# Last blocks of the last attention group straight to TensorE, and the last 512 rows in two interleaved halves

## The chip, the cores and the metric

The kernel runs on one core of one Trainium2 chip. The metric is the time of the device in microseconds (us), lower is better. The core has four computing engines, each with a queue of its own that is worked off in order: TensorE (PE) multiplies matrices, VectorE (DVE) and ScalarE (ACT) work element by element and read the results of TensorE from PSUM, GpSimd (POOL) works element by element in SBUF. SyncE (SP) only issues DMAs; GpSimd issues DMAs as well, among them those that add what they carry to their destination. Engines wait for one another by semaphores.

## The reference

One layer of graph attention over 8 frames of 2048 rows with 256 channels, 8 heads of 32 channels, and a mask that is the same for all frames:

```python
scores = jnp.einsum('fnhd,fmhd->fhnm', q, k) / jnp.sqrt(jnp.asarray(D, x.dtype))
mask = (adj > 0)[None, None, :, :]
scores = jnp.where(mask, scores, jnp.asarray(-1000000000.0, x.dtype))
attn = jax.nn.softmax(scores, axis=-1)
t = jnp.einsum('fhnm,fmhd->fnhd', attn, v).reshape(F, N, C)
x = _layernorm(x + t, ln1_g, ln1_b)
h = jax.nn.relu(jnp.einsum('fnc,cd->fnd', x, w1) + b1)
f_out = jnp.einsum('fnd,dc->fnc', h, w2) + b2
x = _layernorm(x + f_out, ln2_g, ln2_b)
...
x = _layernorm(x + _L0_gnn_ref(x, adj, ...), axis=-1)
```

So each row passes three layer norms: after the attention (with the input added), after the feed-forward part, and after the input has been added once more. All is in float32.

## The kernel before, in words

The queries are taken in chunks of 512 rows, `qc`, four to a frame. A chunk is done in two groups `g` of four heads, and a group in 16 blocks `mb` of 128 keys. So there are 8 x 4 x 2 x 16 = 1024 items. The main loop has one step for each item:

- `scores` of the item two steps ahead: four matmuls on TensorE (L230), and two operations of VectorE that add the mask and write the tile `p` (L233);
- `exponentials` of the item one step ahead: one activation of ScalarE in place (L237);
- `values` of this item: four matmuls that add up over the group's 16 blocks in PSUM (L249);
- `add_up`: the softmax sums. The 16 tiles `p` of a group are first added to each other: blocks 3, 6, 8, 11, 13, 15 onto block 0 by GpSimd (L271, `POOLED`), blocks 4, 7, 10 onto 1 and 5, 9, 12 onto 2 by DMAs that GpSimd issues (L268, `MOVED`); block 14 stays alone. `denominator` then multiplies the four tiles that are left with ones on TensorE (L310), a "term" of four matmuls each. In the very last group blocks 13 and 15 are terms of their own (`ENDED`), six terms in all. The sum is copied by ScalarE (`dT`, L312), transposed, and VectorE takes the reciprocal.

All else is written as generators, kept in a list `fill` with a start step and a due step. Before each step `advance` resumes them: `yield BANK` asks for a PSUM bank, and is granted when TensorE has credit left in the step or the earliest due step has come; `yield n` waits n steps; only one generator holds the spare bank. The program's text so made is the order of every engine's queue; nothing is reordered later.

`outcome` divides a chunk's attention by its sums (L345), and GpSimd issues a DMA that adds the input rows to y (L334). `tail` follows: the first norm (`norm`: statistics on VectorE, L278 and L279; power and products on GpSimd, L282 to L286; scaling on ScalarE, L289), `feed_forward` (transposes, the activation L410 that writes `turned`, W1 on TensorE with a relu on ScalarE, L423, W2 with a sum on VectorE, L436; y times g1 and plus be1 and b2 on GpSimd, L412 and L414), the second norm, g2 and be2 on GpSimd (L355, L357), a DMA that adds the input again (L359), the third norm, and the output DMA by SyncE (L362). A tail may start 10 steps after a chunk's `outcome` could, and is due 16 steps later. It thus runs in the next chunk's loop, except for what is left of the second-last chunk's tail when the loop ends.

The last chunk has `finish` in the place of `outcome` and `tail`. Its norms are done by `norm_halves`, two row tiles after the other two (statistics L372, L373; GpSimd L375, L376; L378 makes the bias `nb`; scaling L382), but its feed-forward part takes the four tiles at once. The input rows are loaded eight steps before the loop's end. `finish` has no points at which it gives way to the tail after its feed-forward part, so the last part of that tail is recorded behind all of `finish`.

Of the kernel before, what the change touches and what calls it, by code (L numbers as in the profile page):

```python
# [10 lines left out]
F32 = mybir.dt.float32  # L11
# [8 lines left out]
P = 128  # L20
# [41 lines left out]
def fast_path(ctx, tc, cst, x, adj, out, RS):  # L62
# [52 lines left out]
    def take(shape, dt):  # L115
        live.pop(0)
        live.append(ld.tile(shape, dt, name="in"))
        return live[-1]
# [139 lines left out]
    MOVED = ((1, 4, 7, 10), (2, 5, 9, 12))  # L258
    ALONE = 14

    ENDED = (13, 15)
    SUM = 4

    def add_up(item):
        f, qc, g, mb = item
        for chain in MOVED:
            if mb in chain[1:]:
                nc.gpsimd.dma_start(PT[f, qc, g, chain[0]], PT.pop(item), accum_op=ALU.add)  # L268
        if mb in POOLED[1:] and not ((f, qc, g) == items[-1][:3] and mb in ENDED):
            first = PT[f, qc, g, POOLED[0]]  # L270
            nc.gpsimd.tensor_tensor(first, first, PT.pop(item), ALU.add)  # L271


    def norm(t):
        mv = small.tile([P, TPC, nc.vector.BN_AGGR_DIM], F32, name="mv")
        for j in range(TPC):
            st = small.tile([P, nc.vector.BN_STATS_DIM], F32, name="st")
            nc.vector.bn_stats(st, t[:, j, :])  # L278
            nc.vector.bn_aggr(mv[:, j, :], st)  # L279
            yield 1  # L280
        rs = small.tile([P, TPC], F32, name="rs")
        nc.gpsimd.tensor_scalar(rs, mv[:, :, 1], EPS, 1.0, op0=ALU.add, op1=ALU.mult)  # L282
        nc.gpsimd.tensor_tensor(rs, rs, cst["mhalf"], ALU.pow)  # L283
        nb = small.tile([P, TPC], F32, name="nb")
        nc.gpsimd.tensor_tensor(nb, mv[:, :, 0], rs, ALU.mult)
        nc.gpsimd.tensor_scalar(nb, nb, -1.0, 1.0, op0=ALU.mult, op1=ALU.mult)  # L286
        yield 2
        for j in range(TPC):
            nc.scalar.activation(t[:, j, :], t[:, j, :], AF.Identity, bias=nb[:, j:j + 1], scale=rs[:, j:j + 1])  # L289
            yield 1  # L290

    def rows(v):
        return v[:, None, :].to_broadcast([P, TPC, C])

    def denominator(f, qc, g, ready):
        grp = (f, qc, g)
        terms = [PT.pop((f, qc, g, ALONE))] + [PT.pop((f, qc, g, chain[0])) for chain in MOVED + (POOLED,)]
        if (f, qc, g) == items[-1][:3]:
            terms[3:3] = [PT.pop((f, qc, g, b)) for b in ENDED]
        yield BANK  # L300
        ps = bank()
        for n, term in enumerate(terms):
            if n:
                yield MORE
            while n == len(terms) - 1 and state["now"] < ready:
                yield WAIT
            state["credit"] -= 4 * CH
            for h in range(4):
                r = D * h
                nc.tensor.matmul(ps[r:r + D, :], cst["ones"], term[:, h, :], start=(n == 0), stop=(n == len(terms) - 1))  # L310
        dT = op.tile([P, CH], F32, name="dT")
        nc.scalar.copy(dT, ps)  # L312
        yield 1
        yield BANK
        ps = bank()
        transposes(ps, [dT[:, j::TPC] for j in range(TPC)])
        if g == 0:
            RC[f, qc] = op.tile([P, TPC, H], F32, name="rc")
        rc = RC[f, qc]
        den = ps.rearrange("p (j c) -> p j c", c=P)[:, :, ::D]  # L320
        nc.vector.reciprocal(rc[:, :, 4 * g:4 * g + 4], den)
        nc.vector.tensor_tensor(RS[:, 0], RS[:, 0], den, ALU.add)
        nc.vector.tensor_tensor(RS[:, 1], RS[:, 1], den, ALU.min)
        if g == 1:
            begin = items.index((f, qc, g, LAST)) + SUM + 2
            start(begin, outcome(f, qc) if (f, qc) != (F - 1, NCK - 1) else finish(f, qc), begin)

    def outcome(f, qc):
        yield ROOM
        state["tails"] += 1  # L330
        xin = x[f, qc * CH:(qc + 1) * CH, :].rearrange("(p j) c -> p j c", p=P)
        y = yp.tile([P, TPC, C], F32, name="y")
        yield from divide(f, qc, y)
        nc.gpsimd.dma_start(y, xin, accum_op=ALU.add)  # L334
        begin = items.index((f, qc, 1, LAST)) + SUM + 2
        start(begin + 10, tail(f, qc, y, xin), begin + 26)

    def divide(f, qc, y):
        rc = RC.pop((f, qc))
# [6 lines left out]
                                    ps.rearrange("p (j h d) -> p j h d", h=4, d=D),  # L346
                                    rc[:, :, 4 * gg:4 * gg + 4, None].to_broadcast([P, TPC, 4, D]), ALU.mult)

    def tail(f, qc, y, xin):
        yield from norm(y)  # L350
        yield from feed_forward(y)
        yield 1
        z = y
        yield from norm(z)
        nc.gpsimd.tensor_tensor(z, z, rows(cst["g2r"]), ALU.mult)  # L355
        yield 1
        nc.gpsimd.tensor_tensor(z, z, rows(cst["be2r"]), ALU.add)  # L357
        yield 1
        nc.gpsimd.dma_start(z, xin, accum_op=ALU.add)  # L359
        yield 7  # L360
        yield from norm(z)
        nc.sync.dma_start(out[f, qc * CH:(qc + 1) * CH, :].rearrange("(p j) c -> p j c", p=P), z)  # L362
        state["tails"] -= 1


    def norm_halves(t):
        both = []
        for h in range(0, TPC, 2):
            mv = small.tile([P, 2, nc.vector.BN_AGGR_DIM], F32, name="mv")
            for j in range(2):  # L370
                st = small.tile([P, nc.vector.BN_STATS_DIM], F32, name="st")
                nc.vector.bn_stats(st, t[:, h + j, :])  # L372
                nc.vector.bn_aggr(mv[:, j, :], st)  # L373
            rs = small.tile([P, 2], F32, name="rs")
            nc.gpsimd.tensor_scalar(rs, mv[:, :, 1], EPS, 1.0, op0=ALU.add, op1=ALU.mult)  # L375
            nc.gpsimd.tensor_tensor(rs, rs, cst["mhalf"][:, 0:2], ALU.pow)  # L376
            nb = small.tile([P, 2], F32, name="nb")
            nc.vector.scalar_tensor_tensor(nb, mv[:, :, 0], -1.0, rs, op0=ALU.mult, op1=ALU.mult)  # L378
            both.append((h, rs, nb))
        for h, rs, nb in both:  # L380
            for j in range(2):
                nc.scalar.activation(t[:, h + j, :], t[:, h + j, :], AF.Identity, bias=nb[:, j:j + 1], scale=rs[:, j:j + 1])  # L382

    def finish(f, qc):
        y = yp.tile([P, TPC, C], F32, name="y")
        xr, xb = state["rows"], take([P, TPC, C], F32)
        yield from divide(f, qc, y)
        nc.vector.tensor_tensor(y, y, xr, ALU.add)
        norm_halves(y)
        nc.vector.tensor_tensor(xb, xr, rows(cst["be2r"]), ALU.add)  # L390
        yield from feed_forward(y)
        z = y
        norm_halves(z)
        for h in range(0, TPC, 2):
            nc.vector.tensor_tensor(z[:, h:h + 2], z[:, h:h + 2], rows(cst["g2r"])[:, h:h + 2], ALU.mult)
            nc.vector.tensor_tensor(z[:, h:h + 2], z[:, h:h + 2], xb[:, h:h + 2], ALU.add)
        norm_halves(z)
        dst = out[f, qc * CH:(qc + 1) * CH, :].rearrange("(p j) c -> p j c", p=P)
        for h in range(0, TPC, 2):
            nc.sync.dma_start(dst[:, h:h + 2], z[:, h:h + 2])  # L400

    def feed_forward(y):
        yield TURNED
# [37 lines left out]
    def start(t, gen, due):  # L441
        fill.append([t, gen, 1, due])
        fill.sort(key=lambda e: e[3])
# [108 lines left out]
    for t, (f, qc, g, mb) in enumerate(items):  # L552
        if g == 1 and mb % 2 and (f + 1 < F or qc + 1 < NCK):
            load_mask(f + (qc + 1) // NCK, (qc + 1) % NCK, mb // 2)
        for what, *which in NEXT.get(t % FRAME, []):
            to = f if what is ask and which[0] else f + 1
            if to < F:
                at = (0, 0, 0) if what is turn else (which[0], 0, 0) if what is ask else (0, which[1], which[0] * TPC)
                start(t, what(to, *which), t + 3 * MB if what is turn else items.index((to, *at)) - LEAD - 1)
        if t == len(items) - MB // 2:  # L560
            state["rows"] = take([P, TPC, C], F32)
            nc.sync.dma_start(state["rows"], x[f, qc * CH:(qc + 1) * CH, :].rearrange("(p j) c -> p j c", p=P))
        if t:
            advance(t)

        if t + 1 < len(items):
            exponentials(items[t + 1])
        if t + LEAD < len(items):
            nf, _, ng, nmb = items[t + LEAD]
            t0 = t  # L570
            while (nf, nmb // TPC, ng) not in V:
                advance(t0, finish=True)
                t0 += 1
            scores(items[t + LEAD])
        values(items[t])
        add_up(items[t])
        if mb == LAST:
            start(t + 2, denominator(f, qc, g, t + SUM), t + SUM + 4)
    t = len(items)
    state["side"] = None  # L580
    while fill:
# [238 lines left out]
```

## Time and profile before

| what | us |
|---|---|
| median of 3 runs | 3248.77 (3247.61 to 3251.02) |
| profiled execution, its own time | 3242.05 |
| its span | 3240.0 |
| mask addition on VectorE, L233, mean of 2048 | 1.219 |
| exponential on ScalarE, L237, mean of 1024 | 1.910 |
| addition on GpSimd, L271, mean of 382 | 4.791 |
| DMA p<-p, median from issue to landing, 384 of them | 10.5 |
| DMA y<-in_x_dram, the same, 62 of them | 8.0 |

The span is the time from the first to the last instruction of one profiled execution; times of day below are from the start of this span. A line of the timeline gives start, length, engine, line, operation, the tile written and the tiles read, how many instructions are merged in it, and in brackets how long the engine was idle before and who ended the wait. "x8" in matmul lines counts the records of four matmuls in float32. The chain of waits goes back from the last instruction, at each step to what released it. A line such as L54 is a helper's, so W1 and W2 are told apart by the tiles read: `turned,w1s` and `w2s,hT`.

### The profile page before, as it was taken

The page shows a single profiled execution, that of the slowest core. Times are in us where ns is not written, and L with a number is a line of the kernel's source. Part 1 is how long each engine was busy: PE and PEld are TensorE (multiplying, and loading weights), DVE is VectorE, ACT ScalarE, POOL GpSimd, SP SyncE. Part 2 cuts the span into 40 slices and gives each one's busy share as a digit, 9 for nine tenths or more (in the row PEclk, how much of TensorE's full clock was granted, in tenths as well). Part 3 has the DMA queues.
Part 4 walks back from the last instruction along what each step waited for, and adds up shares of the span by engine and source line. Part 5 has one row for each costly group of instructions (what it writes and reads, how often), then busy time and mean ns, then how long its engine had stood idle before and what let it go on. Part 6 is the DMA issues. An engine that isn't in the chain of part 4 may idle for free.

```text
span 3240.0 us, 68306 instructions
## 1 busy us (share of the span) xinstructions
PE 3101.0 (96%) x28948; PEld 976.0 (30%) x28948; DVE 2739.5 (85%) x3203; ACT 2435.5 (75%) x1937; POOL 2593.3 (80%) x1357
## 2 busy tenths in 40 slices
PE   7899999999999999999999999999999999998994
PEld 4222333323332233322333323323233323332221
DVE  4888888888888888888988888888888888888994
ACT  3667778778778777778777778777778777777773
POOL 0568888788878888788887888888888788878894
PEclk8899999999999999999999999999999999999997
DMA  9688779778879788788788879878788878877773
GB/s 322 147 179 190 182 175 202 176 174 200 181 176 205 171 190 193 158 195 200 177 181 175 184 181 220 177 167 197 175 192 194 180 171 201 181 171 160 168 160 78
DMA packets 153384, 591.57 MB, mean 183 GB/s; under 512 B 15056, under 2 KB 67792, under 8 KB 103920
## 3 DMA queue, kind: packets, MB, share of 16 engines
q0 software_dynamic: 64560, 435.85, 67.2%
q1 hardware_dynamic: 87696, 149.98, 13.1%
q8 instruction: 229, 3.75, 0.4%
q10 hardware_dynamic: 816, 1.31, 0.1%
q14 instruction: 83, 0.68, 0.1%
HBM read 146.67 MB, written 37.75 MB: 57 GB/s over the span
## 4 chain that ended last, share of the span: by engine, by line
PE 75%; DVE 8%; POOL 5%; DMA 4%; issue 4%; ACT 2%; DVEq 0%; ACTq 0%; POOLq 0%
PE s L230 28%; PE x L249 24%; PE x L54 13%; DVE p L233 6%; PE x L310 6%; PE x L95 4%; DMA p<-p 3%; POOL p L271 2%; ACT p L237 2%; DMA mask<-md 1%; POOL y L357 1%; DVE st L278 1%; POOL y L355 0%; POOL y L414 0%; POOL y L412 0%
## 5 line engine op out<-in xcount | busy, mean ns | idle before, releaser
L233 DVE TENSOR_TENSOR p<-s,mask 128x1024 f32<-128x1024 f32 x2048 | 2410.5, 1219 | 360.3 <-PE s L230 202.9
L237 ACT ACTIVATE p<-p 128x2048 f32<-128x2048 f32 x1024 | 1956.3, 1910 | 510.2 <-DVE p L233 456.7
L271 POOL TENSOR_TENSOR p<-p 128x2048 f32<-128x2048 f32 x382 | 1829.5, 4791 | 216.0 <-ACT p L237 213.8
L230 PE MATMUL s<-qT,kT 32*128 32x512 f32 x8192 | 1171.2, 641 | 34.1 <-DVE p L233 29.1
L249 PE MATMUL x<-p,v 128*32 128x512 f32 x8192 | 1092.9, 606 | 16.7 <-ACT p L237 16.7
L268 POOL DMA_DIRECT2D p<-p x384 | 360.1, 957 | 305.5 <-ACT p L237 95.5
L230 PEld LDWEIGHTS s<-qT,kT 32*128 32x128 f32 x8192 | 320.5, 183 | 637.8 <-DVE p L233 580.1
L249 PEld LDWEIGHTS x<-p,v 128*32 128x32 f32 x8192 | 161.3, 108 | 796.4 <-issue 302.6
L310 PE MATMUL x<-p,ones 128*32 128x512 f32 x2016 | 261.1, 594 | 15.9 <-POOL p L271 9.7
L289 ACT ACTIVATE y<-y,nb,rs 128x256 f32<-128x256 f32 x372 | 219.2, 590 | 46.1 <-POOL nb L286 46.1
L54 PE MATMUL x<-in,wqkv 128*32 128x512 f32 x1888 | 243.5, 592 | 0.0
L278 DVE BATCH_NORM_STATS2 st<-y 128x6 f32<-128x256 f32 x372 | 155.2, 417 | 6.2 <-DMA y<-in_x_dram 6.2
L54 PE MATMUL x<-w2s,hT 128*32 128x256 f32 x2048 | 122.8, 381 | 3.3 <-DVE y L436 2.3
L54 PE MATMUL x<-turned,w1s 128*32 128x512 f32 x992 | 122.9, 592 | 0.4 <-ACT in L166 0.4
L54 PEld LDWEIGHTS x<-wqkv,in 128*32 128x32 f32 x3584 | 102.2, 110 | 63.5 <-issue 59.0
L54 PE MATMUL x<-wqkv,in 128*32 128x128 f32 x3584 | 117.2, 273 | 0.0
L310 PEld LDWEIGHTS x<-p,ones 128*32 128x32 f32 x2016 | 64.1, 110 | 171.4 <-issue 136.0
L54 PEld LDWEIGHTS x<-in,wqkv 128*32 128x32 f32 x1888 | 61.7, 110 | 140.9 <-issue 113.7
L283 POOL TENSOR_TENSOR rs<-rs,mhalf 128x4 f32<-128x4 f32 x93 | 97.1, 1044 | 7.7
L54 PEld LDWEIGHTS x<-w2s,hT 128*32 128x32 f32 x2048 | 66.1, 110 | 76.5 <-issue 30.3
L414 POOL TENSOR_TENSOR y<-y,be1b2r 128x1024 f32<-128x1024 f32 x32 | 85.4, 2667 | 0.6
L355 POOL TENSOR_TENSOR y<-y,g2r 128x1024 f32<-128x1024 f32 x31 | 82.7, 2668 | 1.2 <-ACT y L289 1.2
(117 smaller groups left out, 1333.1 us busy)
## 6 DMA issues: line engine op xcount, KB each, us to landing
p<-p POOLq DMA_DIRECT2D x384, 1024.0 KB, 10.5
in<-xd SPq DMA_DIRECT2D x87, 512.0 KB, 10.7
mask<-md SPq DMA_DIRECT2D x248, 128.0 KB, 8.0
y<-in_x_dram POOLq DMA_DIRECT2D x62, 512.0 KB, 8.0
p<-in_adj_dram SPq DMA_DIRECT2D x16, 1024.0 KB, 9.7
out_dram<-y SPq DMA_DIRECT2D x31, 512.0 KB, 6.4
in<-in_x_dram SPq DMA_DIRECT2D x29, 512.0 KB, 15.9
xd<-in SPq DMA_DIRECT2D x28, 512.0 KB, 10.9
```

Of the source, the lines that this page charges most:

```text
L54: nc.tensor.matmul(out[r:r + D], lhsT[:, r:r + D], rhs, start=start, stop=stop)
L95: nc.tensor.transpose(ps[:, j * P:(j + 1) * P], s, ident)
L230: nc.tensor.matmul(ps2[half][:, j, :], KT[f, mb // TPC, g][r:r + D, (mb % TPC) * P:(mb % TPC + 1) * P], QT[f, qc, g][r:r + D, :], start=Tr ...
L233: nc.vector.tensor_tensor(pt[:, 2 * half:2 * half + 2, :], ps, MK[f, qc, mb // 2][:, mb % 2, None, :].to_broadcast([P, 2, CH]), ALU.add)
L237: nc.scalar.activation(PT[item], PT[item], AF.Exp, scale=1.0 / math.sqrt(D))
L249: nc.tensor.matmul(O[grp][r:r + D, :], V[f, mb // TPC, g][:, mb % TPC, r:r + D], PT[item][:, h, :], start=(mb == 0), stop=(mb == LAST))
L268: nc.gpsimd.dma_start(PT[f, qc, g, chain[0]], PT.pop(item), accum_op=ALU.add)
L271: nc.gpsimd.tensor_tensor(first, first, PT.pop(item), ALU.add)
L278: nc.vector.bn_stats(st, t[:, j, :])
L283: nc.gpsimd.tensor_tensor(rs, rs, cst["mhalf"], ALU.pow)
L289: nc.scalar.activation(t[:, j, :], t[:, j, :], AF.Identity, bias=nb[:, j:j + 1], scale=rs[:, j:j + 1])
L310: nc.tensor.matmul(ps[r:r + D, :], cst["ones"], term[:, h, :], start=(n == 0), stop=(n == len(terms) - 1))
```

## The change

It has three parts, and touches only the last group and the last two chunks.

1. In the last group blocks 11 to 15 are not added up: no GpSimd addition of block 11, no DMA of block 12. `denominator` has eight terms there instead of six, in the order 0, 11, 12, 2, 13, 14, 1, 15, each with the step before which it must not come, and it starts three steps before the loop's end and not two steps after.
2. The second-last chunk's tail may start 5 steps after its `outcome` could (10 before) and is due 3 steps later (16 before). Its norms do two row tiles to a step (`per=2`) instead of one.
3. `finish` makes two generators `half_rows`, for two row tiles each, and resumes them in turn through all stages: norm, products, transposes, W1, W2, norm, g2 and be2, norm, output DMA. The products with g1 and the sum with be1 and b2 go to tiles of the input rows. The input rows plus be2 (`xb`) are made by GpSimd two steps before the loop's end, where VectorE made them in `finish`.

```diff
-    ENDED = (13, 15)
+    ENDED = MB - 5
...
-            if mb in chain[1:]:
+            if mb in chain[1:] and not ((f, qc, g) == items[-1][:3] and mb >= ENDED):
...
-        if mb in POOLED[1:] and not ((f, qc, g) == items[-1][:3] and mb in ENDED):
+        if mb in POOLED[1:] and not ((f, qc, g) == items[-1][:3] and mb >= ENDED):
...
-        terms = [PT.pop((f, qc, g, ALONE))] + [PT.pop((f, qc, g, chain[0])) for chain in MOVED + (POOLED,)]
+        blocks = [ALONE] + [chain[0] for chain in MOVED + (POOLED,)]
+        late = {len(blocks) - 1: ready}
         if (f, qc, g) == items[-1][:3]:
-            terms[3:3] = [PT.pop((f, qc, g, b)) for b in ENDED]
+            blocks = [POOLED[0], 11, 12, MOVED[1][0], 13, 14, MOVED[0][0], 15]
+            late = {n: len(items) - k for n, k in ((2, 2), (3, 1), (4, 1), (5, 0), (6, 0), (7, 0))}
...
-        start(begin + 10, tail(f, qc, y, xin), begin + 26)
+        if (f, qc) == (F - 1, NCK - 2):
+            start(begin + 5, tail(f, qc, y, xin, 2), begin + 8)
+        else:
+            start(begin + 10, tail(f, qc, y, xin), begin + 26)
...
+    def half_rows(h, y, xr, xb, yT, hT, dst):
...
+        nc.vector.tensor_tensor(y, y, xr, ALU.add)
+        if h:
+            yield
+        found = half_stats(y)
+        yield
+        half_norm(y, *found)
+        nc.gpsimd.tensor_tensor(xr, y, row2(cst["g1r"]), ALU.mult)
+        nc.gpsimd.tensor_tensor(xr, xr, row2(cst["be1b2r"]), ALU.add)
+        yield
+        ps = bank()
+        transposes(ps, [y[:, j, a * P:(a + 1) * P] for a in range(2) for j in range(2)])
+        for a in range(2):
+            nc.scalar.activation(yT[:, a, q], ps[:, a * 2 * P:(a + 1) * 2 * P], AF.Identity,
+                                 bias=cst["be1c"][:, a:a + 1], scale=cst["g1c"][:, a:a + 1])
+        yield
...
+            nc.scalar.activation(hT[:, d, q], ps[:, d * 2 * P:(d + 1) * 2 * P], AF.Relu, bias=cst["b1s"][:, d:d + 1], scale=1.0)
+        yield
...
+        nc.vector.tensor_tensor(z, ps.rearrange("p (b c) -> p b c", c=C), xr, ALU.add)
+        found = half_stats(z)
+        yield
+        half_norm(z, *found)
+        yield
+        nc.vector.tensor_tensor(z, z, row2(cst["g2r"]), ALU.mult)
+        nc.vector.tensor_tensor(z, z, xb, ALU.add)
+        found = half_stats(z)
+        yield
+        half_norm(z, *found)
+        nc.sync.dma_start(dst[:, own], z)
...
+        both = [half_rows(h, y, xr, xb, yT, hT, dst) for h in range(2)]
+        while both:
+            for e in list(both):
+                if next(e, both) is both:
+                    both.remove(e)
...
+        if t == len(items) - 2:
+            nc.gpsimd.tensor_tensor(xb, xr, rows(cst["be2r"]), ALU.add)
...
-        if mb == LAST:
+        if mb == LAST and t + 1 < len(items):
             start(t + 2, denominator(f, qc, g, t + SUM), t + SUM + 4)
+        if t == len(items) - 3:
+            start(t, denominator(f, qc, g, t), t)
```

`half_stats` and `half_norm` are the statistics and the scaling of `norm_halves`, for one half each.

## The prediction

> **What bounds the kernel now.** The page's first part:
>
> ```profile
> span 3240.0 us, 68306 instructions
> PE 3101.0 (96%) x28948; PEld 976.0 (30%) x28948; DVE 2739.5 (85%) x3203; ACT 2435.5 (75%) x1937; POOL 2593.3 (80%) x1357
> ```
>
> These shares are those of a long uniform loop and say nothing on its end, where the change lies. The built program of the changed kernel has the same instructions in the same order on all engines up to block 11 of the group before the last, so only the last 128 us of the span can change. There the chain of work that ended last is:
>
> ```profile
> 3173.61 2.30 POOL y L414
> 3175.91 7.17 DMA p<-p
> 3183.12 3.69 PE s L310 x32
> 3186.83 0.59 ACT dT L312
> ...
> 3220.96 2.32 POOL y L357
> 3223.27 0.29 issue
> 3223.56 5.85 DMA y<-in_x_dram
> 3229.44 0.44 DVE st L278
> ```
>
> (start, length, what.) The last multiplication with the values starts at 3173.88, but its softmax sums reach ScalarE (dT) only at 3186.83: they wait for the add of block 12, whose DMA GpSimd issues late, behind additions. From there to the end of the span lie 53.2 us: the last 512 rows, and after them the tail of the 512 rows before, which waits for L357 and its DMA. Then the timeline of the loop:
>
> ```profile
> 3084.36 1.06 PE L249 MATMUL x<-p,v 128*32 128x512 f32 x8
> ...
> 3085.24 1.91 PE L54 MATMUL x<-w2s,hT 128*32 128x256 f32 x32
> ...
> 3088.15 1.07 PE L249 MATMUL x<-p,v 128*32 128x512 f32 x8
> ...
> 3112.27 4.83 DVE L233 TENSOR_TENSOR p<-s,mask 128x1024 f32<-128x1024 f32 x4
> ...
> 3112.65 0.86 POOL L334 DMA_DIRECT2D y<-in_x_dram  x1 [1.49 <-DVE y L345]
> ...
> 3117.29 4.84 DVE L233 TENSOR_TENSOR p<-s,mask 128x1024 f32<-128x1024 f32 x4 [0.19 <-ACT y L289]
> ```
>
> DVE adds the mask back to back, a block in 2.4 to 2.5 us: a plain step is DVE's. In a step that also holds 16 matmuls of 256 columns TensorE is the limit: 3088.15 - 3084.36 = 3.79 us. So a step costs max(2.5, 2.05 + TensorE's extra work), plus DVE's extra work where DVE limits. The instructions of L334 in a window around its last issue answer:
>
> ```profile
> DMA to landing us min/median/max: 9.6/9.6/9.6
> ```
>
> Those rows of y are complete at 3112.65 + 9.6 = 3122.25.
>
> **What the Trainium skill says.** "DMA: Bandwidth & Descriptors", section Queues, rings and completion order: each DMA engine consumes descriptors in ring order. The trace agrees: L334's transfer, behind a 1 MB p<-p transfer issued at 3110.25, took 9.6 us; the same kind at 3223.56, with nothing ahead, took 5.9. "TensorE: Matmul & The Clock Gate", Part 1: idle for about 3.4 us halves the clock, about 3.4 us of work restores it. The stretches of two us agree; the number before the last two is the granted clock:
>
> ```profile
> 3188.00:3190.00 2.00, 1.19 (x10) 0.99 (x9) 1.75 (x9) 0.00 (x0) 0.00 (x0) 1.00 0.00 0
> 3192.00:3194.00 2.00, 0.00 (x0) 0.00 (x0) 1.27 (x5) 0.00 (x0) 0.44 (x2) 0.50 0.00 0
> 3202.00:3204.00 2.00, 2.00 (x24) 0.60 (x20) 0.00 (x0) 1.17 (x2) 1.92 (x2) 1.00 0.00 0
> ```
>
> The last matmul before the gap ended at 3189.2, steady work began again at 3198.2. "SBUF — State Buffer", section SBUF: two separate sides: a DVE operation with two SBUF inputs and a GpSimd operation that reads SBUF exclude each other. The trace shows it once: L378 took 2.29 us beside L357, elsewhere 0.16.
>
> **Part 1, the sums.** Blocks 11 and 12 of the last group are no longer added up: one L271 (4.83 us) leaves GpSimd and one DMA (issue 1.2, landing 7.2) goes, and TensorE gets two more terms of four matmuls. A term is 0.86 us in the chain of waits. The built order has three terms after the multiplication of block 13, two after 14, three after 15. From the start of the last multiplication to dT there were 3186.83 - 3173.88 = 12.95 us; now 1.06 + 3 x 0.86 + 0.2 = 3.8. Saved: 9.1. The DMA of block 10, the last one left, is issued near 3176 and lands 8 to 10 us later, before TensorE asks at 3193. Tail work shares GpSimd with it; 8 us of slack cover that.
>
> **Part 2, the tail of the preceding rows sooner.** Its first statistics now stand on DVE behind the mask of block 11, where they were behind that of the next group's block 0. That is the costly place: DVE reaches it at 3117.1 and waits until 3122.3 for y. Masks, exponentials and scores of all later blocks queue behind. I walked the built queues step by step with the durations of the rows above (statistics 0.55 a pair, L289 0.55, exponential 1.91). Times are starts of the value multiplication.
> - Block 10 to the last group's block 0: 15.5 us before (3117.09 to 3132.58). Now 5.2 for the wait, 3 x 0.55 for statistics that were later, some 0.3 for four L289 before two exponentials: 22.6, +7.1.
> - Block 0 to 9: before 25.7 (to 3158.27). Now the two transposes and two activations make a step of 3.3; one term 3.0; three terms in one step 2.05 + 2.58 = 4.6; W1 twice and W2 twice four steps of 3.8 (the measured W2 step); the dT transpose 2.7; three statistics pairs and the reciprocal 4.0. Sum 32.8, +7.1. W1 was there before, spread thinner; W2 (3.7 us), its two L436 on DVE (0.69 each) and the second norm's statistics stood after the loop. The L436 hide under TensorE here.
> - Block 9 to 15: before 15.6 (to 3173.88). Now two statistics pairs (1.1) and eight L289 instead of four between the last exponentials, the second of two norms crowding in: 17.8, +2.2.
> The last multiplication starts 16.4 later, at 3190.3; with part 1, dT starts at 3194.1 instead of 3186.83. The norm's GpSimd steps, L412, L414, the addition to the residual rows (moved from DVE L390) and L357 find GpSimd free of what TensorE needs: 3 us or more of slack at each. The tail's DMA is issued near 3195, lands near 3201, and no one waits for it any more. No SP transfer changes place.
>
> **Part 3, the last rows in halves.** From dT on, d+ in us, durations from the same operations of before. First half: addition done at d+4.0, statistics 5.25, GpSimd's power and nb 6.4, two activations 7.7, transposes 8.4, turned copies (two of 0.55) 9.6, W1 16 matmuls of 256 columns mostly at half clock 12.6. The relu stands on ScalarE behind the second half's normalization, and that one's power stands on GpSimd behind the first half's two products (1.3 each, a half of L412's 2.36 and a bit): 7.7 + 2.6 + 1.0 + 0.3 + 1.1 = d+12.7. Then relu 13.8, W2 15.1, sum and statistics 17.3, normalization 19.8, product and sum (behind the second half's statistics) 22.5, statistics 23.7. The second half follows: normalized 25.0, product and sum 26.3, statistics and power, last nb at d+28.75. Before, the last nb (L378) began at 3220.99 = d+34.2: interleaving saves 5.4.
> The preceding tail is still recorded last on DVE, GpSimd and ScalarE, so its final norm still ends the program: from its first statistics to the end 3240.0 - 3229.44 = 10.56. But its DMA is long in: it starts at d+28.8 where it started 8.4 after the last nb. Saved: 8.5. End at d+39.3 instead of d+53.2: -13.9.
>
> **Sum.** -9.1 + 16.4 - 13.9 = -6.6 us. The profiled execution lay at 3242.05 around its span of 3240.0; the median of the runs is 3248.77, 6.7 us above it, and I subtract from that: 3242.2. What cannot be told from no change is 0.2% of this, 6.5 us: the forecast lies on that border.
>
> **Unknown costs.** TensorE idles from 3118.1 to 3124.6 in the new stall, 6.5 us; the clock should fall. Cost between 0 (DVE limits anyway when it comes back) and 3 (a window longer than seen); my walk through the old kernel's queues ended 0.2 to 1 late, so I take the two as cancelling. Exclusion of DVE and GpSimd in the halves (L357 is gone, powers of 0.72 beside L430): 0 to 2, taken 0. The stall itself: it ends with the DMA's landing, 3119 if the two transfers share the engines evenly (-3), 3124 (+2).
>
> **Rivals.**
> - The gain is eaten up: cold clock 3 and port exclusion 1 on top, -2.6 to -4: 3245.5. For it: both show in the trace. Against: DVE's limit hides part.
> - Gain larger: y lands at 3119 and the stall is 2; -9.8: 3239.0. Against: the 9.6 us is measured with the same transfers ahead.
> - Slower: the clock stays halved in the stretch from block 0 to 9. A step then costs 2.05 us more; four of them cost 8.2 and the gain is gone, and from seven steps on (14.35 - 6.6 = +7.8) it is slower by over 0.2%: 3256.5, with eight 3258.6. For it: TensorE starts that stretch after a gap, and waits on ScalarE in its first two steps. Against: on full work it came back within 3.8 us.
> - That the tail does not end sooner at all: true of its place in the queues, and in the sum.
>
> **Numbers.** As worked out (3239 to 3246) 0.45, eaten up 0.2, larger 0.2, slower 0.15. The likeliest lies half on either side of the border, a little more beyond it counting its long downward side: faster 0.26 + 0.2 + 0.04, same 0.18 + 0.16, slower 0.16. Range 3236 to 3252: the larger gain with 3 us more below, and above the loss of the whole gain with a slow clock for five steps (10.2 - 6.6 = +3.6); the slow case proper stays outside, with the last of the large one.
>
> **What would show it.** Right: a wait of DVE's L278 for y<-in_x_dram near 3117, 5 us; the last value multiplication near 3190; dT within 4 us of it; no wait for DMA p<-p there; last nb 29 us after dT, L278 right behind it; span near 3233. Wrong: y landed before DVE asks; steps of 5 us or more after the stall at a granted clock of 0.5; hT of the first half not held by the second half's normalization; a wait for the DMA of block 10.

## The result, and the profile after

| | before | after |
|---|---|---|
| median of the runs | 3248.0 (22 runs, 3239.89 to 3252.86) | 3243.33 (22 runs, 3234.61 to 3248.29) |
| ratio, with its 95% interval | | 0.9986 (0.998 to 0.9991) |
| profiled execution, its span | 3240.0 | 3244.1 |

The changed kernel is faster by 4.7 us in the medians (by the interval 3 to 6.5). The two spans stand the other way round: each is one execution, and the long loop ahead of the change lasted 6.1 us longer in the profiled execution after. Therefore I compare ends from a common point. The ScalarE copy dT at the end of the second-last chunk (3102.71 before, 3108.85 after) lies ahead of the first instruction that the change moves. Shifting each trace so that these copies coincide gives this table; all times are on the clock of the kernel before.

| | last multiplication with the values | dT of the last group | last nb of the last rows | end |
|---|---|---|---|---|
| before | 3173.88 | 3186.83 | 3220.99 | 3240.00 |
| after | 3190.35 | 3194.03 | 3227.32 | 3237.96 |
| forecast | 3190.3 | 3194.1 | 3222.9 | 3233.4 |

The page after begins with

```profile
span 3244.1 us, 68406 instructions
```

and its chain of waits, from the stall on VectorE to the end (start, length, what), with the lines that answer to those of before:

```profile
3118.78 9.49 DMA y<-in_x_dram
...
3128.36 0.44 DVE st L278
...
3197.53 2.62 PE x L315 x24
3200.17 0.59 ACT dT L317
...
3213.26 0.37 ACT hT L417
3213.68 1.93 PE s L54 x16
...
3232.74 0.71 POOL rs L381
3233.63 0.34 DVE st L278
```

The DMA p<-p and GpSimd's L414 ahead of dT are gone from it: dT comes straight from TensorE's last terms. The tail's last DMA is gone too: the third norm of the tail (L278 at 3233.63) now follows the last rows' own power (L381). The stall is new. The timeline shows it, and the one place where the last rows are slower than I had worked out (L386 makes nb of the first half, L425 is its sum behind W2):

```profile
3128.36 0.43 DVE L278 BATCH_NORM_STATS2 st<-y 128x6 f32<-128x256 f32 x1 [5.13 <-DMA y<-in_x_dram]
...
3206.85 0.16 DVE L386 SCALAR_TENSOR_TENSOR nb<-mv,rs 128x2 f32<-128x2 f32 x1 [0.88 <-POOL rs L381]
...
3209.60 1.27 POOL L405 TENSOR_TENSOR in<-in,be1b2r 128x512 f32<-128x512 f32 x1
...
3211.23 0.71 POOL L381 TENSOR_TENSOR rs<-rs,mhalf 128x2 f32<-128x2 f32 x1
...
3212.17 1.09 ACT L388 ACTIVATE y<-y,nb,rs 128x256 f32<-128x256 f32 x2 [1.97 <-DVE nb L386]
3213.17 0.45 ACT L417 ACTIVATE hT<-s,b1s 128x256 f32<-128x256 f32 x1
...
3213.68 1.93 PE L54 MATMUL s<-turned,w1s 128*32 128x256 f32 x16 [1.95 <-ACT hT L417]
...
3216.59 2.72 PE L54 MATMUL x<-w2s,hT 128*32 128x256 f32 x32
...
3219.45 0.69 DVE L425 TENSOR_TENSOR y<-x,in 128x512 f32<-128x512 f32 x1 [7.32 <-PE x L54]
```

Read it upwards from the matmuls at 3213.68. These, for the second of W1's two results, wait 1.95 us for the relu of the first (L417): both results lie in one PSUM bank, and the program lets TensorE write the second only when ScalarE has read the first. The Trainium skill has the rule behind this ("PSUM — Partial Sum Buffer", section Summary: rules for kernel authors): to read PSUM while a matmul runs, aim the matmul at another bank. The wait is in the trace; that it goes with a second bank is tested below. This relu stands on ScalarE behind the second half's normalization (L388), which waits for the power (L381), which stands on GpSimd behind the first half's two products (L404, L405). Ahead of all this TensorE stood idle from 3202.5 to 3207.7, and from 3206 to 3218 its granted clock is 0.50. The Trainium skill, on the page that the prediction names ("TensorE: Matmul & The Clock Gate", Part 1), puts an idle window of about 3.4 us before such a fall; here the clock fell sooner, about 2 us after the last matmul (mean 0.65 from 3204 to 3206). W2 of the first half, 32 records, takes 2.72 us, nearly all at that clock; of the second half, in two pieces at full clock, 0.61 + 1.50.

### The profile page after: what moved, and what is told of

It is laid out like the page before. It is cut to its first block, busy times and chain, and to the rows that moved or that the text cites. A ratio compares the mean times of both kernels' runs of the same rounds, so it can differ in the third digit from the quotient of the medians.

```text
span 3244.1 us, 68406 instructions
## 1 busy us (share of the span) xinstructions
PE 3109.4 (96%) x28996; PEld 979.0 (30%) x28996; DVE 2735.7 (84%) x3203; ACT 2435.8 (75%) x1941; POOL 2592.2 (80%) x1358
## 4 chain that ended last, share of the span: by engine, by line
PE 75%; DVE 7%; POOL 5%; issue 4%; DMA 4%; ACT 2%; DVEq 0%; POOLq 0%; ACTq 0%
PE s L230 27%; PE x L249 24%; PE x L54 14%; PE x L315 6%; DVE p L233 6%; PE x L95 4%; DMA p<-p 3%; POOL p L271 2%; ACT p L237 1%; DMA mask<-md 1%; POOL y L365 1%; DVE st L278 1%; POOL y L363 0%; POOL y L461 0%; POOL y L459 0%
## 5 line engine op out<-in xcount | busy, mean ns | idle before, releaser
L233 DVE TENSOR_TENSOR p<-s,mask 128x1024 f32<-128x1024 f32 x2048 | 2409.3, 1218 | 372.7 <-PE s L230 209.9
L249 PE MATMUL x<-p,v 128*32 128x512 f32 x8192 | 1096.0, 607 | 16.7 <-ACT p L237 16.4
L315 PE MATMUL x<-p,ones 128*32 128x512 f32 x2080 | 268.2, 594 | 17.9 <-POOL p L271 11.1
L290 ACT ACTIVATE y<-y,nb,rs 128x256 f32<-128x256 f32 x372 | 218.7, 590 | 40.4 <-POOL nb L287 40.4
L278 DVE BATCH_NORM_STATS2 st<-y 128x6 f32<-128x256 f32 x372 | 154.9, 416 | 5.1 <-DMA y<-in_x_dram 5.1
L363 POOL TENSOR_TENSOR y<-y,g2r 128x1024 f32<-128x1024 f32 x31 | 82.5, 2663 | 5.3 <-ACT y L290 5.3
## 6 DMA issues: line engine op xcount, KB each, us to landing
p<-p POOLq DMA_DIRECT2D x383, 1024.0 KB, 10.4
```

What stands on the lines that cost most here:

```text
L233: nc.vector.tensor_tensor(pt[:, 2 * half:2 * half + 2, :], ps, MK[f, qc, mb // 2][:, mb % 2, None, :].to_broadcast([P, 2, CH]), ALU.add)
L249: nc.tensor.matmul(O[grp][r:r + D, :], V[f, mb // TPC, g][:, mb % TPC, r:r + D], PT[item][:, h, :], start=(mb == 0), stop=(mb == LAST))
```

## The experiments

Each kernel was timed beside the kernel before. The table has the places as above (shifted in the same way), and the ratio of the times to the kernel before.

| run | last values | dT | last nb | end | ratio (95%) |
|---|---|---|---|---|---|
| part 1 alone | 3175.97 | 3180.47 | 3221.15 | 3244.36 | 1.0005 (0.9997 to 1.0014) |
| part 2 alone | 3189.09 | 3199.51 | 3232.91 | 3239.86 | 0.9993 (0.9985 to 1.0001) |
| part 3 alone | 3173.85 | 3186.89 | 3221.20 | 3246.63 | 1.0018 (1.001 to 1.0025) |
| parts 1 and 3 | 3175.29 | 3178.98 | 3220.08 | 3246.91 | 1.0017 (1.0008 to 1.0026) |
| parts 1 and 2 | 3190.40 | 3194.09 | 3227.75 | 3234.56 | 0.9981 (0.9974 to 0.9987) |
| tail two steps later | 3189.36 | 3193.04 | 3227.99 | 3238.60 | 0.9991 (0.9983 to 1.0) |
| in step, two banks | 3189.44 | 3193.13 | 3221.82 | 3232.40 | 0.9973 (0.9965 to 0.998) |
| in step, one bank | 3190.59 | 3194.27 | 3223.46 | 3234.08 | 0.9974 (0.9964 to 0.9984) |
| final norm amid | 3190.39 | 3194.08 | 3231.01 | 3236.07 | 0.9981 (0.9974 to 0.9987) |
| residual rows by DVE | 3189.57 | 3193.25 | 3227.03 | 3237.60 | 0.9987 (0.998 to 0.9994) |
| in step, norm later amid | 3190.60 | 3194.29 | 3224.07 | 3229.04 | 0.9963 (0.995 to 0.9977) |
| the same, residual by DVE | 3189.60 | 3193.28 | 3221.82 | 3227.48 | 0.9959 (0.9946 to 0.9973) |

In every run the ratio, times 3247 us, gives 0.7 to 2.7 us more gain, or so much less loss, than the trace's end. The likeliest reason, which no run shows, is that the one profiled execution of the kernel before, to which all ends are compared, had an end some 1.5 us shorter than usual. Differences between two experiments are free of that, but not of the scatter of single executions: in the changed kernel and the four runs that differ from it only behind the loop (the two in step, and the two with the norm amid that keep the residual DMA) the last values stand anywhere from 3189.44 to 3190.60. A difference of 1 us between two places of this table is therefore no finding by itself.

### The three parts one by one

My theory was the sum: -9.1 for part 1, +16.4 for part 2, -13.9 for part 3. The rival: the parts are no terms of a sum, since each decides where the tail of the preceding rows stands among the last rows.

Part 1 alone: the kernel before with the edits in `ENDED`, `add_up` and `denominator` of the diff.

> The kernel before with the sums alone changed: blocks 11 to 15 of the last group go to TensorE as they are; the tail of the preceding rows and the last rows stay as they were. Theory (the sum's first term): dT follows the last value multiplication within 5 us, where it stood 12.95 us behind it, and the end comes 9 us sooner, ratio 0.9972 to the kernel before. Rival: the tail of the preceding rows, which this kernel still finishes after the loop on GpSimd and by a DMA, does not come sooner when dT does; dT gains 9 us, the end 3 or less, ratio 0.999 to 1.0.

dT came 6.4 us sooner, not 9: the terms put the last values off by 2.1, and 0.61 us of wait for a DMA p<-p was left. The end came 4.4 later by the trace; in the medians no gain is left. In the kernel before GpSimd did the tail's product with g2 amid the last rows:

```profile
3205.66 2.37 POOL L355 TENSOR_TENSOR y<-y,g2r 128x1024 f32<-128x1024 f32 x1 [1.20 <-ACT y L289]
```

With part 1 alone it is in the chain of waits at the very end, behind everything:

```profile
3187.30 1.90 PE x L54 x16
3189.22 0.70 ACT hT L426
3189.96 3.27 PE s L54 x56
...
3227.94 0.50 ACT y L289
3228.51 2.34 POOL y L358
3230.93 2.35 POOL y L360
3233.28 0.29 issue
3233.57 5.70 DMA y<-in_x_dram
```

The second half of the tail's W1, its relu and W2 (first three lines) now follow dT. In the kernel before, that half of W1 and its relu stood ahead of the last values, and W2 (at 3175.65) ran while dT was awaited. From dT to the last nb it now takes 40.7 us instead of 34.2. And the tail's second norm ends behind the last rows, where it ended amid them, with it the product (L358, L355 before). So the wait of 13 us ahead of dT was not empty: it covered the tail's work. The rival's reason holds, and the ratio lies just above its range.

Part 2 alone: the edits in `norm`, `outcome` and `tail`.

> The kernel before with only the tail of the preceding rows begun sooner; sums and last rows as before. Theory (the sum's second term): the last value multiplication starts 16 us later, DVE stands for about 5 us at its statistics for y<-in_x_dram, and of this some 8.5 us are won back because the tail's last DMA is in when the last rows are done, and some 4 to 8 because GpSimd has less to do at the end and dT waits less: ratio 1.001 to 1.002. Rival: dT still waits 13 us behind the last value multiplication, since the DMA of block 12 still stands behind GpSimd's additions: ratio 1.0025 or more.

The last values came 15.2 later, dT 12.7, the last nb 11.9, and the end 0.1 sooner. dT stood 10.4 us behind the last values, so the win there was 2.5, not 4 to 8. No DMA is awaited there any more, so the rival is out: TensorE runs its six terms in one go, for more than half of that time at a clock of 0.50 (3190 to 3198):

```profile
3194.07 7.71 PE L312 MATMUL x<-p,ones 128*32 128x512 f32 x48 [0.70 <-ACT oT L253]
```

The larger part came back at the end: from the last nb to the end it took 6.95 us instead of 19.01, because not only the tail's DMA had landed, but its third norm had passed as well. The theory holds in its direction; that the end comes a little sooner than before was in neither's range.

Part 3 alone: `finish` and `half_rows`, and `xb` on GpSimd.

> The kernel before with only the last 512 rows in two halves (and xb on GpSimd). Theory (the sum's third term, without what needs the sooner tail): the distance from dT to the last nb of the last rows falls from 34.2 us, to 28.75 by my walk or to the 33.3 that the changed kernel shows; the tail's last DMA is still awaited, so the end moves by -1 to -5: ratio 0.9985 to 0.9997. Rival: the addition for xb, now on GpSimd between the last additions of blocks, puts off the DMA of block 12 and with it dT by 2 to 5 us: ratio 1.0 to 1.0012.

Slower by 0.18%, which neither foresaw. dT stood where it was (the rival is out), and from dT to the last nb it took 34.31 us instead of 34.16: nothing won by the halves. From the last nb to the end 25.4 instead of 19.0: `finish` now gives way nowhere while the halves run, so the end of the tail's second norm, the product with g2, the addition of be2, the DMA and the third norm stand behind all of it.

Parts 1 and 3, without part 2:

```diff
-        if (f, qc) == (F - 1, NCK - 2):
-            start(begin + 5, tail(f, qc, y, xin, 2), begin + 8)
-        else:
-            start(begin + 10, tail(f, qc, y, xin), begin + 26)
+        start(begin + 10, tail(f, qc, y, xin), begin + 26)
```

> The changed kernel with the tail of the preceding rows begun where it began before (parts 1 and 3 without part 2). It tells what part 2 is worth when the other two are there. Theory (my sum): part 2 costs 16.4 us in the loop and brings 8.5 at the end, so without it the end comes 4 to 8 us sooner than in the changed kernel, ratio 0.9965 to the kernel before. Rival: without part 2 the tail's work on GpSimd, its W2 matmuls and its last DMA all stand after the loop behind the last rows, and the end comes later than in the changed kernel: ratio 0.9995 to 1.002.

The rival holds: without part 2 the other two make the kernel slower by 0.17%. dT comes 7.9 us sooner than in the kernel before, but from dT to the last nb it takes 41.1 us, since the tail's W1 and W2 follow dT here too, and 26.8 us lie between the last nb and the end.

Parts 1 and 2, with the last rows as before:

> The changed kernel with the last 512 rows as before (parts 1 and 2, without the halves). The single parts gave +1.6, -2.3 and +5.8 us, so their sum is not that of the whole. In the run of part 2 alone the last rows took 33.4 us from dT to their last nb, unhalved, in the changed kernel 33.3, and the tail's final norm had passed before, so that the end came 7.0 us behind the last nb instead of 10.6. Theory (the halves bring nothing here and put the tail's final norm behind everything): dT within 4 us of the last value multiplication, 33.4 us to the last nb, end 7 us behind: 3 to 4 us sooner than the changed kernel, ratio 0.9975. Rival (my sum, interleaving saves 5.4 us): 2 to 5 us later than the changed kernel, ratio 0.9992 to 1.0.

The theory holds by the trace: 3.4 us sooner than the changed kernel; the ratios, 0.9981 against 0.9986, agree in sign, though their intervals overlap. What differs is the place of the tail's third norm. Here, in the old `finish`, its statistics, power and four activations stand amid the last rows, and the run ends at 3240.0:

```profile
3217.05 2.07 ACT L290 ACTIVATE y<-y,nb,rs 128x256 f32<-128x256 f32 x4
```

In the changed kernel, which ends at 3244.1, they come last:

```profile
3237.80 2.07 ACT L290 ACTIVATE y<-y,nb,rs 128x256 f32<-128x256 f32 x4 [2.99 <-POOL nb L287]
```

So the gain of the change is that of parts 1 and 2 together, which need each other; part 3, as it is, brings 0.4 us between dT and the last nb, which is within the scatter, and takes 3.8 behind it.

### Why the last rows took 33.3 us from dT

Both halves in step (the second no longer one stage behind the first), and a bank for each result of W1:

```diff
-        if h:
-            yield
         found = half_stats(y)
...
-        ps = bank()
         for d in range(2):
+            ps = bank()
             for a in range(2):
-                columns(ps[:, d * 2 * P:(d + 1) * 2 * P], ...)
+                columns(ps[:, 0:2 * P], ...)
...
```

> The changed kernel with both halves in step from the first addition on (the second half's power stands on GpSimd ahead of the first half's products) and a PSUM bank for each of the two results of W1. Theory for the 4.5 us that the last rows took longer than I worked out: the relu of the first half waits on ScalarE for the second half's normalization, and the second half of W1 for that relu; with both taken away dT to the last nb takes 30 to 31.5 us instead of 33.3, ratio 0.9979. Rival: the granted clock of 0.50 and GpSimd beside DVE made the difference, and it stays at 33 us: ratio 0.9986.

28.69 us: better than my theory's 30 to 31.5. The second half's power now stands ahead of the products on GpSimd, and W1 runs through:

```profile
3201.89 0.70 POOL L381 TENSOR_TENSOR rs<-rs,mhalf 128x2 f32<-128x2 f32 x1
...
3202.82 1.27 POOL L402 TENSOR_TENSOR in<-y,g1r 128x512 f32<-128x512 f32 x1 [0.23 <-ACT y L388]
...
3204.80 3.58 PE L54 MATMUL x<-turned,w1s 128*32 128x256 f32 x32
```

The rival is out in its other part as well: L381 still takes 1.14 us beside L429 here, as it did beside L431 in the changed kernel. The half clock ends sooner (0.98 from 13.5 us behind dT on, in the changed kernel 0.97 from 17.8 on). How much of the 4.6 us that makes, the run with the tail two steps later (below) tells: its last rows have the order of the changed kernel, but W2 of its first half ran at nearly full clock.

```profile
3207.62 0.16 DVE L386 SCALAR_TENSOR_TENSOR nb<-mv,rs 128x2 f32<-128x2 f32 x1 [1.78 <-POOL rs L381]
...
3217.37 1.96 PE L54 MATMUL x<-w2s,hT 128*32 128x256 f32 x32
...
3219.48 0.69 DVE L425 TENSOR_TENSOR y<-x,in 128x512 f32<-128x512 f32 x1 [6.56 <-PE x L54]
```

From the first nb to the sum behind W2 it takes 11.9 us here, 12.6 in the changed kernel (3206.85 to 3219.45). So the clock makes about 0.7 us of the 4.6, and the rest is order and bank.

The same with the first half of the edit only, one bank as in the changed kernel:

> The changed kernel with both halves in step, but with one PSUM bank for the two results of W1 as in the changed kernel. It parts the two causes that the run with step and banks took away together (dT to last nb 28.69 us instead of 33.29). Theory: the order on GpSimd and ScalarE is the larger part, since the relu no longer stands behind a late normalization; the shared bank costs about 1 us a half: dT to last nb 30 to 31 us, ratio 0.9978. Rival: the shared bank is the cause, since W1's second result waits for the relu of the first in either order: 32 us or more, ratio 0.9984.

29.19 us: putting the halves in step makes 4.1 of the 4.6 us, the bank 0.5. The first figure is that of the whole new order, on VectorE and TensorE as well, and not of the late relu alone. The second is no larger than the scatter, and the ratios, 0.9974 and 0.9973, are the same. W1's second result waits for the relu here too, but 0.6 us at a time, since the relu is no longer late. The theory holds: the shared bank did its larger harm only while something else held the relu up.

### The tail's third norm

The halves give way after each step, and the tail waits 3 steps instead of 7 for its DMA:

```diff
                 if next(e, both) is both:
                     both.remove(e)
+            yield 1
...
-        yield 7
+        yield 7 if per == 1 else 3
```

> The changed kernel with the tail's final norm placed amid the steps of the last rows, not behind them (the halves give way after each step, and the tail yields 3 steps instead of 7 for its DMA, which has landed by then). Theory: the end comes 5.5 to 7 us behind the last nb instead of 10.6, while four statistics and activations more stand among those of the last rows and put off the last nb by 1 or 2: 2 to 4 us sooner, ratio 0.9976. Rival: the statistics and activations cost on the path what they cost behind it: ratio 0.9985 to 0.999.

The end comes 5.06 us behind the last nb, a little better than expected, but the last nb 3.7 later: 1.9 us are left. The statistics now stand ahead of the division, and the first of them waits for the tail's DMA:

```profile
3199.07 0.43 DVE L278 BATCH_NORM_STATS2 st<-y 128x6 f32<-128x256 f32 x1 [0.87 <-DMA y<-in_x_dram]
```

Between theory and rival. The place matters, so I put the norm later, and joined it with the halves in step: `yield 6` in the place of 3, and both edits of the run in step.

> The halves in step, two PSUM banks, and the tail's final norm amid the last rows, but later among them than in the run before (its statistics stand on DVE behind both halves' first statistics, where DVE waits for W1 and W2 for 9 us; its power on GpSimd behind the products, its activations on ScalarE where it waits). Theory: the norm is hidden, dT to last nb stays at 28.7 to 29.5, and the end comes 5.1 us behind it: 10 to 11 us sooner than the changed kernel, ratio 0.9956. Rival: as in the run where it stood earlier, it puts off the last nb by 3 us or more: ratio 0.9967 to 0.997.

```profile
3213.50 1.08 ACT L290 ACTIVATE y<-y,nb,rs 128x256 f32<-128x256 f32 x2
...
3221.02 1.07 ACT L290 ACTIVATE y<-y,nb,rs 128x256 f32<-128x256 f32 x2
...
3222.12 0.34 SPq L370 DMA_DIRECT2D out_dram<-y  x1
...
3226.32 1.62 SPq L433 DMA_DIRECT2D out_dram<-y  x2
```

The tail's output (L370) is issued ahead of the last rows' (L433). dT to the last nb takes 29.78 us, 1.1 more than in step alone, since two of the norm's four statistics stand ahead of the first two nb on VectorE (the first of these begins 8.0 us behind dT instead of 6.9); the end follows 4.97 behind. 8.9 us sooner than the changed kernel by the trace, 3233.03 us in the median of 5 runs (ratio 0.9963): faster than both kernels, a little less than I expected.

### The stall of 5.13 us

The tail two steps later:

```diff
-            start(begin + 5, tail(f, qc, y, xin, 2), begin + 8)
+            start(begin + 7, tail(f, qc, y, xin, 2), begin + 10)
```

> The changed kernel with the tail begun two steps later (begin+7, due at begin+10): its first statistics then stand on DVE behind a mask that is read after y<-in_x_dram has landed. Theory: the 5.1 us stall and the cold clock behind it go, 2 us of these come back as later transposes, the last value multiplication comes 4 to 6 us sooner and so does the end: ratio 0.997. Rival: the tail's W2, second norm and their GpSimd steps, two steps later, crowd at the end of the loop or behind it, and its last DMA is awaited again: no gain, ratio 0.9985 to 1.0.

The rival's ratio holds. L278 waits only 0.26 us for the DMA, but the last values come only 1.0 us sooner, which the scatter covers. The wait has moved:

```profile
3143.81 1.09 ACT L290 ACTIVATE y<-y,nb,rs 128x256 f32<-128x256 f32 x2 [3.97 <-POOL nb L287]
...
3146.76 1.94 PE L249 MATMUL x<-p,v 128*32 128x512 f32 x8 [3.87 <-ACT p L237]
...
3153.59 2.36 DVE L233 TENSOR_TENSOR p<-s,mask 128x1024 f32<-128x1024 f32 x2 [8.22 <-PE s L230]
```

The tail's normalization (L290) waits on ScalarE for GpSimd, which is working off an addition of the third-last chunk, one of blocks (4.89 us) and that chunk's DMA; behind it on ScalarE stand exponentials, and so the multiplication waits, and in the end VectorE, for 8.22 us. The tail's product and addition (L363 and L365) come only behind dT, ahead of the first half's power on GpSimd, so that from dT to the last nb it takes 35.0 us instead of 33.3. One point of the rival fails: the tail's last DMA is not awaited.

The residual rows loaded ahead of time and added by VectorE:

```diff
-        nc.gpsimd.dma_start(y, xin, accum_op=ALU.add)
+        if (f, qc) == (F - 1, NCK - 2):
+            nc.vector.tensor_tensor(y, y, state["before"], ALU.add)
+        else:
+            nc.gpsimd.dma_start(y, xin, accum_op=ALU.add)
...
+        if t == len(items) - 2 * MB - 4:
+            xr = state["before"] = take([P, TPC, C], F32)
+            nc.sync.dma_start(xr, x[f, qc * CH:(qc + 1) * CH, :].rearrange("(p j) c -> p j c", p=P))
```

> The changed kernel with the residual rows of the preceding tail loaded ahead of time and added on DVE (1.24 us) instead of by the DMA y<-in_x_dram, for which DVE stood 5.13 us. It measures what the stall costs. Theory: 5.1 us of stall and up to 2 us of cold clock go, 1.2 us of addition come, so the last value multiplication and the end come 4 to 6 us sooner: ratio 0.9971. Rival (what the start two steps later showed): the work behind the stall meets other waits, of ScalarE and TensorE for GpSimd, and at most 1.5 us are won: ratio 0.9981 to 0.9988.

The rival's ratio holds: only 0.8 us at the last values, and this too is within the scatter. No one waits for that DMA any more, but the addition, priced at 1.24 us from L388 of the kernel before, took 4.44:

```profile
3112.68 4.74 POOL L271 TENSOR_TENSOR p<-p 128x2048 f32<-128x2048 f32 x1
...
3114.07 4.44 DVE L340 TENSOR_TENSOR y<-y,in 128x1024 f32<-128x1024 f32 x1
```

It ended at 3118.51 (3114.07 + 4.44), 1.09 us behind the end of GpSimd's addition (3112.68 + 4.74 = 3117.42): it stood nearly all that time. That is the exclusion which the Trainium skill describes ("SBUF — State Buffer", section SBUF: two separate sides) for a VectorE operation with two SBUF inputs beside a GpSimd operation that reads SBUF: whichever starts first has the shared ports, and the other blocks for that whole instruction. The trace agrees. The prediction had named this rule; in pricing this edit I left it out. So this run exchanged a wait of 5.13 us for one of some 3.2, and is no measure of the stall.

The last run joins this edit with the best one:

> The three together: halves in step with two banks, the tail's final norm amid them, the residual rows added on DVE. Theory: the gains add, since they lie one behind the other: 14 to 16 us sooner than the changed kernel, ratio 0.9942. Rival: without the stall the tail's last DMA is not in sooner, since GpSimd's queue sets it, and its final norm waits for it amid the last rows: ratio 0.9955, no better than without this edit.

1.6 us sooner by the trace, but 3233.74 against 3233.03 in the medians: the two can't be told apart. The rival's number was right, its reason wasn't: no L278 waits for a DMA amid the last rows, but the addition was held up again (4.43 us). What the stall would bring if it were taken away with nothing put in its place stays open.

## Why the prediction was right, and where it was not

The time as worked out, 3242.2, lies 1.1 us below the median measured, and the direction was right. By the trace the sum was less good: one of its steps failed, and that the time came so near is in part luck. Step by step:

- **Part 1, from the last values to dT.** Forecast 3.8 us, measured 3.68; no wait for the DMA of block 10. Right. But that the end gains by these 9.1 us was only true beside part 2. With part 1 alone the tail's work, which had used the wait, came behind it. The prediction took the wait for empty time; what had been done in it was not asked.
- **Part 2, the last values 16.4 later.** Measured 16.5 (3190.35). The stall was forecast with 5.2 us and took 5.13. TensorE's clock did fall behind it (0.50 from 3130 to 3134, 0.71 to 3138). The three stretches of the walk took 24.0, 32.0 and 17.2 us where 22.6, 32.8 and 17.8 were worked out: the first, with the cold clock, 1.4 more, the other two 1.4 less together. So the two cancelled as they were taken to, but that they did so to 0.1 us is luck.
- **Part 3, "interleaving saves 5.4".** This step failed: it saved 0.9 in the changed kernel, and alone it lost 0.15. The failing place is "then relu 13.8, W2 15.1". The relu began at d+13.0, much as the walk has it. But the walk let both results of W1 be done ahead of it; the second begins only behind it (d+13.5) because of the bank, ends at half clock at d+15.4, its relu at d+16.0, and W2 runs from d+16.4, nearly all at half clock, until d+19.1. The sum with the products began at d+19.3. The runs in step show that the order of the halves is the cause: with it changed, the same stages take 28.69 us with two banks and 29.19 with one. That the first of these is so near the 28.75 of the walk confirms nothing, since the walk was of the other order.
- **Part 3, the end.** From the last nb, with the tail's third norm right behind it, to the end: forecast 10.56 us, measured 10.64. Right as a length, but the 8.5 us saved there are due to part 2 (part 2 alone: last nb to end 6.95, part 3 alone 25.4). And the comparison missed that the old `finish` would have hidden this norm once part 2 had brought it forward: 6.8 us with parts 1 and 2, so that part 3 cost 3.8 where I booked 8.5 in its favour.
- **The total.** By the trace the end moved by -2.0 where -6.6 was forecast; the 4.5 between them are part 3's interleaving. The medians moved by -4.7. By mechanism this is the rival "the gain is eaten up" (-2.6 to -4), but eaten up by the order in `half_rows`, not by the clock in the stall or by excluded ports. That the time came nearer than the working deserves is luck: the medians moved by 2.6 us more than the trace's end, which nothing in the sum foresaw (most likely the one execution of the kernel before that the sum was made against, as said above; not shown), and the median that the sum started from, of 3 runs, came out 0.8 lower in 22.
- **Excluded ports, taken as 0.** Right for the time. That the trace before shows the exclusion only once was a misreading: the power L283 took 1.85 us beside L390, elsewhere 1.03. In the changed kernel L381 took 1.14 us beside L431, where it took 0.69 to 0.71 otherwise, but the nb that needed it stood behind statistics on VectorE anyway.
- **The slow rival** (a halved clock from block 0 to block 9 of the last group) did not come about: from 3138 to 3200 the granted clock was 1.00.

## What to carry to other kernels

The end of a program is one queue per engine, so price a change there by what stands behind what on each queue afterwards, and try each part of a change alone: of these three parts one brings nothing by itself (ratio 1.0005), one loses (1.0018), and the remaining one (0.9993 alone) is the reason why the first pays. A long wait near the end may be the cover for other work; before its removal is counted as a gain, ask where that work goes. When two halves are interleaved, let the short step that others wait for (the power on GpSimd) go ahead of the long ones that nobody waits for yet (the products), and let the last chunk give way to the work that would otherwise follow it: these two edits took the ratio from 0.9986 to 0.9963, in the medians more than the change itself had brought. All this was seen at the end of this one program.

## What was not expected of the hardware

- An addition of 128x1024 float32 on VectorE with both inputs in SBUF took 4.44 and 4.43 us beside GpSimd's addition of 128x2048, and ended 1.09 us behind it both times; without it such an addition took 1.24 (L388 of the kernel before). The mask additions (L233) read PSUM and SBUF, and ran beside the same GpSimd additions at 1.2 us throughout.
- Two results of W1 in one PSUM bank cost TensorE a wait of 1.95 us where the relu was late, of 0.6 us where it was not: the price of such sharing was set by the reader's queue.
- Runs of one kernel spread over 13 us, from 3239.89 to 3252.86 for the kernel before, so that one profiled execution can't carry a sum of a few us.
